# An edge-gated graph layer on one Trainium2 core: aggregation in quarter-width column tiles of TensorE instead of half-width ones

## The chip, the cores and the metric

The kernel runs on one core of a Trainium2 chip. The time is device time of one launch, in microseconds, as the median of the runs; the profile is one execution of the same program recorded by the hardware profiler. Engines are named as in the profile: PE is TensorE's matmul, PEld its weight load, DVE is VectorE, ACT is ScalarE, POOL is GpSimd, SP is SyncE.

## The reference: what is computed

The inputs are `x` (16 batches, 1024 nodes, 256 features) and one sparse matrix `adj` (1024 x 1024, the same for all batches, 9,052 entries that are not zero, 8.8 for a target on average, 19 at most). `adj` stands for both matrices of the layer. Cut to what matters:

```python
pre_u = jnp.einsum('bud,dk->buk', h_t, W1[:d])
pre_v = jnp.einsum('bvd,dk->bvk', h_t, W1[d:])
hidden = jax.nn.relu(pre_u[:, :, None, :] + pre_v[:, None, :, :] + b1)
S = jax.nn.sigmoid(jnp.einsum('buvk,ko->buvo', hidden, W2)[..., 0] + b2[0])
a_t = jnp.einsum('buv,bud->bvd', S * A_a, h_t)
m_t = jnp.einsum('uv,bud->bvd', A_m, h_t) * h_t
z_t = beta1 * h_t + beta2 * (a_t @ Wa + ba) + beta3 * (m_t @ Wm + bm)
```

Only the entries (edges) of `adj` that are not zero count. For each edge from a source u to a target v and each batch there is one gate S; each target sums its sources' rows twice, with weight `adj` (for m) and with weight S times `adj` (for a).

## The kernel before

**Tiling.** The 16 batches go in 4 groups of 4 (`GB`). A block `k` is one group with one tile of 128 targets, so there are 32 blocks. A block has two windows of 64 targets (`W`), and the edges of a window lie in 5 edge tiles (`TW`) of 128 slots each. One pass of the main loop, a step `n`, is one edge tile of one block: 10 steps a block, 320 in all, 64 windows.

**Which edge goes where.** `lists(vt)` sorts each target's edges into the slots. The 64 targets of a window are two halves of 32 (`V`): the lower half fills the slots from the start, the upper half from the end, so the lower half's edges lie in tiles 0, 1, 2 and the upper half's in tiles 2, 3, 4 (`HALVES`). A target's first slot comes from prefix sums that PE makes of the counts (L235 with the fixed matrix `ahead`, L236 with `below`), then from a few DVE operations on one column (L239 to L248). For each edge, `onehot` says which of the half's 32 targets it belongs to (L295).

**A step.** POOL gathers one row of 8 KB an edge from a table in HBM (`fetch`, L480: the rows hold, for 4 batches, the product with W1 and the plain features), into one of 5 buffers `fetched`. PE spreads the targets' product to the edges (`expand`, L494, into `pc`, two buffers). DVE adds the two (`gate`, L510), then does relu, times W2 and the sum for each of 4 batches (L514). ACT makes the weights: `left_adj` (L503) writes one-hot times `adj` for 4 batches, and after the sigmoid (L517) four instructions write the same times the gate (L520). Then `aggregate` (L531) multiplies: the stationary operand is 128 edges x 64 columns (32 targets with weight `adj`, 32 with weight S times `adj`), the moving one is 128 edges x 256 features, one matmul for each batch and each half that the tile has edges of. Two batches share a bank of `acc` side by side: a matmul of 64 columns takes one half of PE's columns, so batches 0 and 1 write partitions 0 to 63 and batches 2 and 3 write partitions 64 to 127; a window has 6 pairs of tile and half, 24 matmuls. These are float32 matmuls, and the trace shows each as two records; L494, in the type fp32r, is shown as one.

**Behind a half.** After tile 2 the lower half is done, after tile 4 the upper one: ACT copies `acc` out (`half_end`, L540), PE turns it over (`turn_over`, L550), ACT copies that to `LT` (L552), DVE multiplies by the targets' own features (`times_h`, L561). `block_end` (L578, L582) multiplies by the two weight matrices and adds. In each block `halves` (L347 with `w_v`, L381, L382, L390, L393) prepares the next block's targets, and in some steps `rows` (L347 with `w_u`, L363) prepares a tile of the table.

**The order of work.** It is written out by hand (`manual_schedule`), and each engine runs its instructions in that order. On PE a step `n` is: `aggregate(n-1)`, then what else the step has (turning over, `block_end`, `halves`, `rows`), then `expand(n+2)`. On DVE it is `gate(n)` and what was put off to it. On POOL, `fetch(n+4)` stands behind `aggregate(n-1)`, whose buffer it takes. On ACT: the copy out of `acc`, the sigmoid, L520 four times, `left_adj(n+1)`.

**Start and end.** The first 95.6 us sort the first edges and fill the first tables. The last window is finished in pieces (`tail`, L606 to L620): for 32 targets at a time it multiplies four batches side by side, in matmuls whose stationary operand is 128 x 32 (the forms `128*32` of L613).

Of the kernel before, what the change touches and what calls it, by code (L numbers as in the profile page):

```python
# [13 lines left out]
P = 128  # L14
# [3 lines left out]
def kernel(  # L18
# [40 lines left out]

    nc = tc.nc  # L60
# [11 lines left out]
    V = 32  # L72
    HALVES = [[0], [0], [0, 1], [1], [1]]
    OFF = [0, V, 2 * V, 4 * V, 5 * V, 6 * V]
    RC = 5 + S
    BIG = float(N * N)
    assert D == 256 and DC == 2 and NW == 2 and S % 8 == 0
# [49 lines left out]

    inw = fixed([P, 1], "inw")
    nc.vector.scalar_tensor_tensor(inw, late, -float(W), row, ALU.mult, ALU.add)
    upper = fixed([P, 1], "upper")  # L130
    nc.vector.tensor_scalar(upper, inw, float(V), None, ALU.is_ge)
    lower = fixed([P, 1], "lower")
    nc.vector.tensor_scalar(lower, inw, float(V), None, ALU.is_lt)
    MID = TW // 2
    until = fixed([P, 1], "until")
    nc.vector.tensor_scalar(until, upper, float((TW - 1 - MID) * P), float((MID + 1) * P), ALU.mult, ALU.add)
    since = fixed([P, 1], "since")
    nc.vector.tensor_scalar(since, upper, float(MID * P), None, ALU.mult)
    base = fixed([P, 1], "base")
    nc.vector.tensor_scalar(base, upper, float(E), None, ALU.mult)  # L140
# [3 lines left out]
    ahead = fixed([P, P], "ahead")  # L144
    below = fixed([P, P], "below")
    hv = fixed([P, 2 * NW, 1], "hv")
    for q in range(2 * NW):
        nc.vector.tensor_tensor(hv[:, q, :], late if q // 2 else soon, upper if q % 2 else lower, ALU.mult)
    nc.vector.memset(below, 0.0)
    for q in range(2 * NW):  # L150
        c = slice(q * V, (q + 1) * V)
        nc.vector.tensor_scalar(ahead[:, c], upto[:, c], row, hv[:, q, :], ALU.is_le if q % 2 else ALU.is_gt, ALU.mult)
        if q % 2:
            nc.vector.tensor_scalar(ahead[:, c], ahead[:, c], -1.0, None, ALU.mult)
            nc.vector.tensor_copy(below[:, c], hv[:, q - 1, :].to_broadcast([P, V]))
# [8 lines left out]
    place = fixed([P, 2, V], "place")  # L164
    nc.vector.tensor_copy(place.rearrange("p k v -> p (k v)"), upto[:, :W])
# [20 lines left out]
    onehot = const.tile([P, NT * NW, OFF[TW]], mybir.dt.bfloat16, name="onehot")  # L186
# [25 lines left out]
    def lists(vt):  # L212
# [22 lines left out]
        nc.tensor.matmul(pw[:, 0:1], ahead, R[:, 0:1], start=True, stop=True)  # L235
        nc.tensor.matmul(pw[:, 1:2], below, R[:, 0:1], start=True, stop=True)  # L236
        yield
        first = R[:, 1:2]
        nc.vector.tensor_tensor(first, pw[:, 0:1], base, ALU.add)  # L239
        from_ = wk.tile([P, 1], FP, name="from", bufs=4)  # L240
        nc.vector.tensor_tensor(from_, pw[:, 1:2], since, ALU.max)
# [51 lines left out]
        for q in range(2):  # L293
            j = slice(q * MID, q * MID + MID + 1)
            nc.vector.tensor_tensor(  # L295
                onehot[:, sl, q * 3 * V:(q + 1) * 3 * V].rearrange("p w (j v) -> p w j v", j=3),
                place[:, q, :].unsqueeze(1).unsqueeze(1).to_broadcast([P, NW, 3, V]),
                col[:, :, j, 4:5].to_broadcast([P, NW, 3, V]), ALU.is_equal)
# [199 lines left out]
    def left_adj(n):  # L498
        k, g, vt, w, j = where(n)
        i = vt * NW + w  # L500
        m = len(HALVES[j])
        lefts[n] = wk.tile([P, m, GB, 2, V], FP, name=f"left{m}", bufs=3 if m == 1 else 1)
        nc.scalar.activation(lefts[n][:, :m, :, 0, :],  # L503
                             onehot[:, i, OFF[j]:OFF[j + 1]].rearrange("p (q v) -> p q v", q=m).unsqueeze(2)
                             .to_broadcast([P, m, GB, V]), AF.Copy, scale=val[:, i, j:j + 1])
# [336 lines left out]
```

## Time and profile before

| what | value |
|---|---|
| median of 3 runs | 1288.98 us (1284.83 to 1293.57) |
| the profiled execution's own time | 1292.69 us |
| its span, from the first to the last instruction | 1290.8 us |
| mean granted TensorE clock over the span | 0.971 |
| first and last `gate` addition on DVE (L510) | 95.6 us, 1268.9 us |
| L514 on DVE, 1280 times | 471.0 us, 423 ns each |
| L510 on DVE, 320 times | 389.2 us, 1216 ns each |
| L494 on PE, 640 times | 247.5 us, 468 ns each |
| L578 on PE, 992 records | 260.9 us, 392 and 379 ns each |

A record of a PE matmul covers its passage through the array, so records overlap: what one costs in a row of them is read from the distance between starts, not from its length. A clock of 1.00 in a row means that TensorE was granted its full clock there. In a list of waits, the columns are the microseconds in total, how often, and the longest. In a table by windows, the number behind an engine's busy time counts its instructions.

### The profile page before, as it was taken

How to read it: one execution, taken by the hardware profiler on the slowest of the kernel's cores; microseconds unless marked ns; L12 is line 12 of the kernel's file. 1: busy time of each engine (PE TensorE's matmuls, PEld its weight loads, DVE VectorE, ACT ScalarE, POOL GpSimd, SP SyncE). 2: the span in 40 equal slices, each digit the busy share in tenths (PEclk: the TensorE clock that was granted, in tenths of full speed). 3: DMA queues.
4: the chain of work that ended last, by engine and by line, in shares of the span. 5: the costliest groups of instructions: out<-in, count | busy, mean ns of one | idle time of the engine just before them, and what ended most of it. 6: DMA issues, size and time to landing. Idle time of an engine off the chain costs nothing. (4 is left out here: it accounts for less than half of the span.)

```text
span 1290.8 us, 21720 instructions
## 1 busy us (share of the span) xinstructions
PE 1193.6 (92%) x6641; PEld 795.9 (62%) x6641; DVE 1089.6 (84%) x3421; ACT 880.4 (68%) x2567; POOL 413.3 (32%) x412
## 2 busy tenths in 40 slices
PE   3838999998979989999999999999999999999996
PEld 3625666665646656666666666666666666666654
DVE  7539878899899888888888898888778999899994
ACT  2426676676757667777777777777677777777773
POOL 0045642352624415222222232222222333233330
PEclk9868999999989989999999999999999999999999
DMA  9469998897898979999998899999998989898892
GB/s 301 154 187 339 313 344 286 279 337 245 280 317 302 341 270 304 332 341 341 335 326 321 323 331 322 318 321 381 345 317 301 338 311 315 297 322 315 318 324 98
DMA packets 151967, 393.37 MB, mean 305 GB/s; under 512 B 16816, under 2 KB 110512, under 8 KB 115632
## 3 DMA queue, kind: packets, MB, share of 16 engines
q0 software_dynamic: 49504, 299.85, 64.7%
q1 hardware_dynamic: 81552, 72.89, 17.5%
q10 hardware_dynamic: 20784, 19.14, 4.8%
q8 instruction: 55, 0.90, 0.3%
q14 instruction: 72, 0.59, 0.1%
HBM read 395.88 MB, written 50.33 MB: 346 GB/s over the span
## 5 line engine op out<-in xcount | busy, mean ns | idle before, releaser
L480 POOL DMA_INDIRECT fetched<-table,uidx x320 | 325.6, 1018 | 747.6 <-PE acc L531 444.5
L514 DVE SCALAR_TENSOR_TENSOR t<-t,w_b 128x256 f32<-128x256 f32 x1280 | 471.0, 423 | 19.4 <-DVE t L510 0.5
L510 DVE TENSOR_TENSOR t<-fetched,pc 128x1024 f32<-128x1024 f32 x320 | 389.2, 1216 | 108.1 <-PE pc L494 69.4
L531 PE MATMUL acc<-fetched,left 128*64 128x256 f32 x3072 | 420.1, 394 | 11.8 <-ACT left L520 11.7
L531 PEld LDWEIGHTS acc<-fetched,left 128*64 128x64 f32 x3072 | 201.7, 138 | 203.2 <-issue 52.1
L520 ACT ACTIVATE left<-left,gt 128x32 f32<-128x32 f32 (+1 forms) x1280 | 313.5, 315 | 10.7
L494 PE MATMUL pc<-X,mark 128*128 128x512 f32 x640 | 247.5, 468 | 19.5 <-DVE t L510 16.5
L517 ACT ACTIVATE gt<-sc,b_b 128x4 f32<-128x4 f32 x320 | 95.2, 297 | 137.2 <-DVE t L514 135.4
L347 PE MATMUL misc<-w_u,hT 128*128 128x256 f32 x512 | 129.3, 401 | 22.6 <-DMA hT<-in_xT_dram 11.7
L494 PEld LDWEIGHTS pc<-X,mark 128*128 128x128 f32 x640 | 118.6, 193 | 40.4 <-DVE t L510 21.0
L503 ACT ACTIVATE left<-onehot,val 128x128 f32<-128x128 bf16 (+1 forms) x320 | 130.3, 407 | 7.8 <-DMA val<-in_adjT_dram,vidx 7.8
L578 PE MATMUL misc<-w_m,LT 128*128 128x256 f32 x496 | 133.6, 392 | 0.0
L540 ACT COPY ev<-acc 128x512 f32<-128x512 f32 x128 | 75.0, 586 | 79.2 <-PE acc L531 79.1
L578 PE MATMUL misc<-w_a,LT 128*128 128x256 f32 x496 | 127.3, 379 | 0.0
L347 PEld LDWEIGHTS misc<-w_u,hT 128*128 128x128 f32 x512 | 97.9, 199 | 43.7 <-issue 11.7
L347 PE MATMUL misc<-w_v,hT 128*128 128x256 f32 x512 | 124.1, 386 | 0.0
L578 PEld LDWEIGHTS misc<-w_m,LT 128*128 128x128 f32 x496 | 88.8, 189 | 33.1 <-issue 23.8
L347 PEld LDWEIGHTS misc<-w_v,hT 128*128 128x128 f32 x512 | 99.8, 195 | 13.8
L305 POOL DMA_INDIRECT val<-in_adjT_dram,vidx x80 | 83.3, 1042 | 76.3 <-DVE eq L280 51.7
L514 DVE DVE_READ_ACCUMULATOR t<-t,w_b 128x1 f32 x1280 | 103.8, 81 | 0.0
L393 ACT CAST X<-misc 64x512 fp32r<-64x512 f32 x128 | 74.4, 581 | 42.7 <-PE misc L390 38.5
L578 PEld LDWEIGHTS misc<-w_a,LT 128*128 128x128 f32 x496 | 94.2, 190 | 12.8
(127 smaller groups left out, 843.0 us busy)
## 6 DMA issues: line engine op xcount, KB each, us to landing
hT<-in_xT_dram SPq DMA_DIRECT2D x40, 512.0 KB, 10.4
table<-in_x_dram ACTq DMA_DIRECT2D x32, 512.0 KB, 8.8
table<-tab SPq DMA_DIRECT2D x32, 512.0 KB, 5.2
h_blk<-in_x_dram SPq DMA_DIRECT2D x31, 512.0 KB, 12.5
out_dram<-h_blk SPq DMA_DIRECT2D x31, 512.0 KB, 5.7
fetched<-table,uidx POOLq DMA_INDIRECT x320, 7.6
key<-in_adjT_dram POOLq DMA_DIRECT2D x6, 512.0 KB, 8.7
whose<-few ACTq DMA_DIRECT2D x32, 40.0 KB, 4.5
```

Of the source, the lines that this page charges most:

```text
L305: nc.gpsimd.indirect_dma_start(out=val[:, i, j:j + 1], out_offset=None, in_=adj_flat, in_offset=bass.IndirectOffsetOnAxis(ap=vidx[:, i, j: ...
L347: nc.tensor.matmul(p[:, bb * D:(bb + 1) * D], hT[:, 2 * h + bb, i, :], wt[:, i, :], start=(i == 0 and not begun), stop=(i == DC - 1), skip ...
L480: nc.gpsimd.indirect_dma_start(out=fetched[n % NF], out_offset=None, in_=table[g], in_offset=bass.IndirectOffsetOnAxis(ap=uidx[:, vt * NW ...
L494: nc.tensor.matmul(pcs[n][:, c], marks[n // TW][:, j * P:(j + 1) * P], cuts[k][:, w, c], start=True, stop=True)
L503: nc.scalar.activation(lefts[n][:, :m, :, 0, :], onehot[:, i, OFF[j]:OFF[j + 1]].rearrange("p (q v) -> p q v", q=m).unsqueeze(2) .to_broad ...
L510: nc.vector.tensor_tensor(t, fetched[n % NF][:, :GD].rearrange("p (b d) -> p b d", b=GB), pcs.pop(n).rearrange("p (b d) -> p b d", b=GB), ...
L514: nc.vector.scalar_tensor_tensor(t[:, b, :], t[:, b, :], 0.0, w2_b, ALU.max, ALU.mult, accum_out=sc[:, b:b + 1])
L517: nc.scalar.activation(gt, sc, AF.Sigmoid, bias=b2_b)
L520: nc.scalar.activation(lefts[n][:, :m, b, 1, :], lefts[n][:, :m, b, 0, :], AF.Copy, scale=gt[:, b:b + 1])
L531: nc.tensor.matmul(accs[q][half * 2 * V:(half + 1) * 2 * V, pair, :], left[:, i, b].rearrange("p k v -> p (k v)"), f[:, GD + b * D:GD + (b ...
L540: nc.scalar.copy(evs[q], accs.pop(q))
L578: nc.tensor.matmul(pz[:, bb * D:(bb + 1) * D], LTs[k][:, bb, c, h, i, :], wt[:, c, :], start=False, stop=(i == 1 and c == DC - 1), skip_gr ...
```

## The change

The half of 32 targets is replaced by a quarter of 16 (`V` is now 16, `Q` is 4, and `U` is the 32 of before). A matmul of `aggregate` has 32 stationary columns (16 targets with each of the two weights), takes a quarter of PE's columns, and the four batches write the four quarters of the partitions of one bank. Quarter q may have edges in tiles q and q+1 (`QUARTERS`), so a window has 8 pairs of tile and quarter, 32 matmuls. Two quarters share a bank (`h, r = divmod(q, 2)`): quarter 0 and 1 the first 256 and the last 256 columns of `acc0`. All else on the path is laid out anew for this: `onehot` has 8 x 16 columns a window and not 6 x 32, `left` is one kind of tile with three buffers (before: three of one size and one of the other), `LT` has another order of its dimensions, and the sorting in `lists` has four prefix sums and not two, with two more DVE operations on one column. On this input every edge still finds a slot in its quarter's tiles, and the rows gathered are as many as before: 9,052 for each group of batches.

```diff
-    V = 32
-    HALVES = [[0], [0], [0, 1], [1], [1]]
+    U = W // 2
+    Q = 4
+    V = W // Q
+    QUARTERS = [[0], [0, 1], [1, 2], [2, 3], [3]]
...
-        nc.tensor.matmul(pw[:, 0:1], ahead, R[:, 0:1], start=True, stop=True)
-        nc.tensor.matmul(pw[:, 1:2], below, R[:, 0:1], start=True, stop=True)
+        for i in range(4):
+            nc.tensor.matmul(pw[:, i:i + 1], sums[:, i].rearrange("p w q v -> p (w q v)"), R[:, 0:1],
+                             start=True, stop=True)
         yield
         first = R[:, 1:2]
-        nc.vector.tensor_tensor(first, pw[:, 0:1], base, ALU.add)
         from_ = wk.tile([P, 1], FP, name="from", bufs=4)
-        nc.vector.tensor_tensor(from_, pw[:, 1:2], since, ALU.max)
+        nc.vector.tensor_scalar(from_, pw[:, 1:2], base, low_, ALU.add, ALU.max)
+        nc.vector.scalar_tensor_tensor(first, from_, high_, pw[:, 0:1], ALU.min, ALU.add)
+        nc.vector.tensor_scalar(from_, pw[:, 2:3], second_, since, ALU.add, ALU.max)
+        nc.vector.tensor_tensor(from_, pw[:, 3:4], from_, ALU.max)
...
-        for q in range(2):
-            j = slice(q * MID, q * MID + MID + 1)
+        for i in range(2):
             nc.vector.tensor_tensor(
...
-        m = len(HALVES[j])
-        lefts[n] = wk.tile([P, m, GB, 2, V], FP, name=f"left{m}", bufs=3 if m == 1 else 1)
+        m = len(QUARTERS[j])
+        o = max(2 * j - 1, 0)
+        lefts[n] = wk.tile([P, 2, GB, 2, V], FP, name="left")
...
-        for i, q in enumerate(HALVES[j]):
-            first = j == (MID if q else 0)
+        for i, q in enumerate(QUARTERS[j]):
+            h, r = divmod(q, 2)
+            first = j == h * MID and r == 0
             if first:
-                accs[q] = psa.tile([P, 2, D], FP, name=f"acc{q}")
-            for b in (0, 2, 1, 3):
-                half, pair = divmod(b, 2)
-                nc.tensor.matmul(accs[q][half * 2 * V:(half + 1) * 2 * V, pair, :],
+                accs[h] = psa.tile([P, 2, D], FP, name=f"acc{h}")
+            for b in range(GB):
+                nc.tensor.matmul(accs[h][b * 2 * V:(b + 1) * 2 * V, r, :],
                                  left[:, i, b].rearrange("p k v -> p (k v)"), f[:, GD + b * D:GD + (b + 1) * D],
-                                 start=(first and pair == 0), stop=(j == (TW - 1 if q else MID)),
-                                 skip_group_check=True)
+                                 start=first, stop=(j == q + 1), skip_group_check=True)
...
-        nc.scalar.copy(LT.rearrange("p a c b k v -> p (a c b k) v")[:, :, v], pt.rearrange("p (i v) -> p i v", v=V))
+        v = slice(w * W + q * U, w * W + (q + 1) * U)
+        r = (w * W + q * U) // V
+        nc.scalar.copy(LT.rearrange("p c b k (r v) -> p r (c b k) v", v=V)[:, r:r + 2],
+                       pt.rearrange("p (r i v) -> p r i v", r=2, v=V))
```

On PE, in a block of the later part of the program, tiles 0 to 2 of a window stand like this before (a name like acc or fetched is a buffer, the size is the output's):

```order
L531 MATMUL acc_6940<-fetched_173,left_6891 64x256 x4
L578 MATMUL misc<-w_m,LT 128x256 x2
L578 MATMUL misc<-w_a,LT 128x256 x2
L494 MATMUL pc<-X,mark 128x512 x2
L531 MATMUL acc_6940<-fetched_174,left_6928 64x256 x4
L550 MATMUL misc<-ident,ev_6843 128x128 x4
L550 MATMUL misc<-ident,ev_6913 128x128 x4
L390 MATMUL misc<-low,swap 128x512
L494 MATMUL pc<-X,mark 128x512 x2
L531 MATMUL acc_6940<-fetched_175,left_6961 64x256 x4
L531 MATMUL acc_7019<-fetched_175,left_6961 64x256 x4
L494 MATMUL pc<-X,mark 128x512 x2
```

and in the changed kernel, where L531 has become L554, L578 L602, L550 L572, L494 L517 and L390 L413:

```order
L554 MATMUL acc_7223<-fetched_176,left 32x256 x4
L602 MATMUL misc<-w_m,LT 128x256 x2
L602 MATMUL misc<-w_a,LT 128x256 x2
L517 MATMUL pc<-X,mark 128x512 x2
L554 MATMUL acc_7223<-fetched_177,left 32x256 x8
L572 MATMUL misc<-ident,ev_7122 128x128 x4
L572 MATMUL misc<-ident,ev_7196 128x128 x4
L413 MATMUL misc<-low,swap 128x512
L517 MATMUL pc<-X,mark 128x512 x2
L554 MATMUL acc_7223<-fetched_178,left 32x256 x4
L554 MATMUL acc_7306<-fetched_178,left 32x256 x4
L517 MATMUL pc<-X,mark 128x512 x2
```

Nothing changes its place; tile 1 (and tile 3, not shown) has eight matmuls where it had four, tiles 0, 2 and 4 have as many as before, and all are 32 columns wide.

On ACT, tiles 0 to 2 of a window before (ev is the copy of acc, L520 the four gated weights of a tile, L503 the one-hot weights of the next tile):

```order
L520 ACTIVATE left_5414<-left_5414,gt 128x32 x4
L503 ACTIVATE left_5451<-onehot,val 128x4x32
L517 ACTIVATE gt<-sc,b_b 128x4
L520 ACTIVATE left_5451<-left_5451,gt 128x32 x4
L503 ACTIVATE left_5484<-onehot,val 128x8x32
L487 CAST mark<-whose 128x640
L517 ACTIVATE gt<-sc,b_b 128x4
L520 ACTIVATE left_5484<-left_5484,gt 128x2x32 x4
L503 ACTIVATE left_5515<-onehot,val 128x4x32
```

and in the changed kernel (L520 has become L543, L503 L527, L517 L540, L487 L510):

```order
L543 ACTIVATE left<-left,gt 128x16 x4
L527 ACTIVATE left<-onehot,val 128x8x16
L540 ACTIVATE gt<-sc,b_b 128x4
L543 ACTIVATE left<-left,gt 128x2x16 x4
L527 ACTIVATE left<-onehot,val 128x8x16
L510 CAST mark<-whose 128x640
L540 ACTIVATE gt<-sc,b_b 128x4
L543 ACTIVATE left<-left,gt 128x2x16 x4
L527 ACTIVATE left<-onehot,val 128x8x16
```

The instructions are as many and stand in the same order; three tiles of five now write 32 columns with each gate, where four wrote 32 and one wrote 64, and two write 16.

More of the change, by code (lines that the diff above doesn't have):

```diff
@@ L145 @@
[L145 to L155, printed above, removed]
+    low_ = fixed([P, 1], "low_")
@@ new lines @@
+    nc.vector.tensor_scalar(low_, mine[:, 1:2], float(P), None, ALU.mult)
+    second_ = fixed([P, 1], "second_")
+    nc.vector.tensor_scalar(second_, mine[:, 2:3], float(P), None, ALU.mult)
+    high_ = fixed([P, 1], "high_")
+    nc.vector.tensor_scalar(high_, second_, -1.0, float(E), ALU.mult, ALU.add)
+    sums = fixed([P, 4, NW, Q, V], "sums")
+    ahead = sums[:, 0].rearrange("p w q v -> p (w q) v")
+    same = hv.rearrange("p w q one -> p (w q) one").to_broadcast([P, NW * Q, V])
+    nc.vector.memset(sums[:, 1:], 0.0)
```

68 lines of the change are left out of this document (39 added, 29 removed).

## The prediction

> **What bounds the kernel now.** I read the page first, for who is busy:
>
> ```profile
> PE 1193.6 (92%) x6641; PEld 795.9 (62%) x6641; DVE 1089.6 (84%) x3421; ACT 880.4 (68%) x2567; POOL 413.3 (32%) x412
> DMA  9469998897898979999998899999998989898892
> GB/s 301 154 187 339 313 344 286 279 337 245 280 317 302 341 270 304 332 341 341 335 326 321 323 331 322 318 321 381 345 317 301 338 311 315 297 322 315 318 324 98
> HBM read 395.88 MB, written 50.33 MB: 346 GB/s over the span
> ```
>
> PE is the busiest, but DVE and the 16 DMA engines are close behind. An average over stages decides nothing, so next comes the table by windows, cut at the first addition of `gate` (95.6), the start of block 10 (507.3, from where no edges are sorted), the end of block 30 (1240.6), and once more inside the long stretch:
>
> ```profile
> core 0: us, PE busy (x) PEld busy (x) DVE busy (x) ACT busy (x) POOL busy (x), PEclk, DMA share, GB/s
> 0.00:95.60 95.60, 49.44 (x193) 40.30 (x193) 50.35 (x139) 32.67 (x44) 16.48 (x22) 0.83 0.69 211
> 95.60:507.30 411.70, 378.33 (x2041) 249.49 (x2043) 368.24 (x1164) 273.99 (x802) 174.72 (x170) 0.96 0.88 307
> 507.30:1240.60 733.30, 726.95 (x4130) 482.81 (x4130) 639.25 (x2020) 550.23 (x1646) 214.84 (x215) 1.00 0.92 324
> 1240.60:1290.80 50.20, 38.88 (x282) 23.30 (x279) 31.76 (x99) 23.51 (x77) 7.25 (x7) 0.94 0.54 182
> ...
> 507.30:865.60 358.30, 355.40 (x2019) 237.03 (x2019) 308.79 (x973) 266.72 (x795) 104.69 (x106) 1.00 0.92 325
> 865.60:1010.10 144.50, 143.54 (x808) 97.42 (x810) 118.67 (x376) 105.43 (x312) 39.14 (x39) 1.00 0.95 335
> 1010.10:1240.60 230.50, 228.01 (x1307) 148.35 (x1303) 211.79 (x673) 178.09 (x540) 71.00 (x71) 1.00 0.89 316
> ```
>
> From 507.3 to 1240.6 PE is busy 726.95 of 733.3 us at full clock: PE sets the pace there, for 57% of the span. Behind it stand DMA (0.92) and DVE (639.25, 87%). From 95.6 to 507.3 nobody is full: PE 92%, DVE 89%, DMA 0.88. Third, the waits, DVE's from 507.3 to 1240.6, then PE's there, then DVE's from 95.6 to 507.3:
>
> ```profile
> DVE t L510 <- PE pc L494: 50.6, 56, 2.6
> DVE low L382 <- ACT X L381: 13.6, 14, 1.0
> DVE t L510 <- DMA fetched<-table,uidx: 8.7, 12, 1.2
> ...
> PE misc L390 <- ACT LT L552: 5.0, 21, 0.2
> PE acc L531 <- ACT left L520: 1.3, 2, 0.8
> ...
> DVE t L510 <- DMA fetched<-table,uidx: 24.0, 6, 16.7
> DVE t L510 <- PE pc L494: 18.2, 18, 2.0
> ```
>
> In the long stretch DVE waits 50.6 us for PE, and PE waits 6.3 us for ACT. That is the picture of a PE that others follow.
>
> [...]
>
> **The aggregation on PE.** [...] Timeline of PE, a tile with one half, the middle tile with two, and the tail, where 32-column matmuls already run four abreast:
>
> ```profile
> 600.13 1.08 PE L531 MATMUL acc<-fetched,left 128*64 128x256 f32 x8
> 601.14 0.50 PE L351 MATMUL misc<-bias_p,unit 128*128 128x512 f32 x1
> ...
> 592.00 1.95 PE L531 MATMUL acc<-fetched,left 128*64 128x256 f32 x16
> 593.88 0.50 PE L351 MATMUL misc<-bias_p,unit 128*128 128x512 f32 x1
> ...
> 1277.61 1.07 PE L613 MATMUL misc<-w_m,LT 128*32 128x256 f32 x16
> 1278.50 1.05 PE L613 MATMUL misc<-w_a,LT 128*32 128x256 f32 x16
> 1279.47 0.38 PE L606 MATMUL misc<-bias_p,unit 128*128 128x256 f32 x1
> ```
>
> Eight records take 1.01 us, sixteen 1.88 us. They run two abreast (64 columns each), so eight more records are four more rounds, and a round is (1.88 - 1.01) / 4 = 0.217 us. In the tail 32 records take 1279.47 - 1277.61 = 1.86 us: as long as eight rounds, so there are four abreast. At that price a tile with one quarter (8 records, two rounds) takes 1.86 - 6 x 0.217 = 0.56 us and a tile with two quarters (16 records, four rounds) 1.86 - 4 x 0.217 = 0.99 us. A window took 4 x 1.01 + 1.88 = 5.92 us and will take 2 x 0.56 + 3 x 0.99 = 4.09 us: 1.83 us less. The saving sits in tiles 0, 2 and 4; tiles 1 and 3 cost what they did. There are 64 windows (L487, once a window, has 64 instructions):
>
> ```profile
> L487 ACT CAST mark<-whose 128x640 fp32r<-128x640 uint8 x64 | 45.4, 709 | 0.0
> L510 DVE TENSOR_TENSOR t<-fetched,pc 128x1024 f32<-128x1024 f32 x320 | 389.2, 1216 | 108.1 <-PE pc L494 69.4 <-DMA fetched<-table,uidx 32.7 <-PE misc L390 1.3
> L480 POOL DMA_INDIRECT fetched<-table,uidx x320 | 325.6, 1018 | 747.6 <-PE acc L531 444.5 <-DVE t L510 216.7 <-DVE t L514 37.7
> ```
>
> So 117 us of PE work go. The unknown is whether four streams that read four different rows of features run abreast as in the tail, where four matmuls read one weight. Bounds: two abreast as in L531 today (8 x 4 rounds a window and not 24, so 8 x 0.217 = 1.74 us more), and four as in L613. I take four: L531's two streams already read different features at the full pace of 0.217.
>
> **What of it reaches the end.** A stretch cannot get shorter than what its other engines need.
>
> From 507.3 on there are 42 windows, 77 us of PE work. In 507.3 to 865.6 DMA is busy 0.92 of 358.3: at a share of 1.00 it needs 330 us, a ceiling of 28.7 us on the gain (PE's: 20 windows, 37). In 865.6 to 1010.1 it is 0.95, a ceiling of 7.2 us. In 1010.1 to 1240.6 DVE is the nearest: 211.79 us busy, and up to 11 us that it loses between its own instructions and to ACT (of the whole stretch's 94 idle us, 51 were PE's and 9 the gather's; the other 34, over 733 us, are 11 in 230), of which the wait for ACT will shrink with PE's. So it needs 219 to 223 us, a ceiling of 8 to 12; I take 12. Sum of the ceilings: 48. None is reached exactly, because fetches have only five buffers and a transfer that comes late is not made up: DVE waits for the gather now already, at times,
>
> ```profile
> 1079.02 1.22 DVE L510 TENSOR_TENSOR t<-fetched,pc 128x1024 f32<-128x1024 f32 x1 [0.81 <-DMA fetched<-table,uidx]
> fetched<-table,uidx POOLq DMA_INDIRECT x320, 7.6
> ```
>
> and a gather takes 7.6 us from issue to landing, more than two steps of 3.5. I take 40 of the 48. What is late next: DVE's additions, behind the gather, and no longer behind `pc`.
>
> From 95.6 to 507.3 there are 20 windows, 37 us of PE work, but DVE waits for PE's `pc` only 18.2 us there; that is the ceiling, and the gather's 24.0 stay. I take 12. The sorting's cost comes off it: two more DVE operations for each of 8 tiles of targets,
>
> ```profile
> L239 DVE TENSOR_TENSOR R<-misc,base 128x1 f32<-128x1 f32 x6 | 0.9, 151 | 0.2 <-PE misc L236 0.2
> L235 PE MATMUL misc<-R,ahead 128*128 128x1 f32 x12 | 2.7, 298 | 0.3 <-DVE R L239 0.3
> L520 ACT ACTIVATE left<-left,gt 128x32 f32<-128x32 f32 x1024 | 245.3, 310 | 8.5
> L520 ACT ACTIVATE left<-left,gt 128x64 f32<-128x64 f32 x256 | 68.2, 337 | 2.1
> L503 ACT ACTIVATE left<-onehot,val 128x128 f32<-128x128 bf16 x256 | 98.8, 386 | 7.8 <-DMA val<-in_adjT_dram,vidx 7.8
> L503 ACT ACTIVATE left<-onehot,val 128x256 f32<-128x256 bf16 x64 | 31.6, 493 | 0.0
> ```
>
> 8 x 2 x 0.15 = 2.4 us, of which 2 of 8 tiles lie in the prologue; and four prefix matmuls for two, 2 x 2 more records of at most 0.3 us for each tile, in all 8 x 4 x 0.3 = 9.6 us of PE if nothing overlapped. Six tiles of them (7 us) fall in this stretch, where PE has just been freed of 37 us; two fall in the prologue (2.4 us at most). I take 2 us here and 1 us in the prologue, with the constants made there; the ends are 0 and 12 together.
>
> From 1240.6 there are two windows, 3.7 us of PE work, and the last tile's matmuls are on the path to the end: 2 us.
>
> Edits that I cost at nothing. ACT gets lighter: the gated weights fall from 4 x 4 x 310 + 4 x 337 ns a window to at most 20 x 310, the one-hot ones from 4 x 386 + 493 to at most 5 x 386 ns, together 0.2 us or more; ACT is at 75% in the long stretch, so this is hidden, and it covers the copies into `LT`, which move 512 elements in 16-element pieces where they had 32; were each a half slower, 128 x 0.3 = 38 us would go on ACT, still under PE's time. `left`, now with three buffers for all tiles, is free again after one step. POOL's and SP's queues keep their order and bytes, so each fetch is only issued earlier, behind an earlier `aggregate`.
>
> Sum: 40 + 12 - 2 - 1 + 2 = 51 us. Against the profiled execution's 1292.7 this gives 1241.7 us. That execution lies 0.3% above the median of the runs, 1289.0; a new median is by the same measure **1238 us**.
>
> **Rivals.** *A, the transfers hold.* If the DMA engines do not go over the share of 0.95 that they held from 865.6 to 1010.1, 358.3 us at 0.92 become 347 (11 gained), the next stretch gains nothing, the third its 12, the first perhaps 5: 28 us, so 1261. For it: gathers that DVE waits for, 346 GB/s of HBM over the span. Against it: one slice of 32 us moved 381 GB/s, above all three stretches' 316 to 335. [...]
>
> *B, slower: the quarters do not run abreast.* If four different moving operands share the array's inputs so that only two run at once, a window costs 1.74 us more; over 42 windows where PE is the bound that is 73 us, and some 35 in the first stretch: 1395 us. It decides at 64 / 24 = 2.67 abreast, where 64 records of a window take the 24 rounds of today. Against it: the tail's 1.86 us for 32 records.
>
> *C, no change.* PE is only followed closely, and DVE or the gather's round trip (five buffers) sets the pace, so the freed time turns into waits: 1289. Against it: the 50.6 us for which DVE waits for PE.
>
> *D, all of PE's part comes out.* DMA takes the higher load without delay and the long stretch loses 64 us (77 less 13 for DVE's own), the first 18, the end 3, less 3: 82 us, 1207.
>
> **Chances and range.** My forecast 0.58, A 0.22, D 0.10, C 0.05, B 0.05. The range from 1212 to 1264 takes in the forecast and A and leaves out B, C and most of D. A measurement of this kernel can tell about 1% (13 us) from no change. Faster by more: the forecast, D and nearly all of A, 0.88; within 1%: C and the rest of A, 0.07; slower: 0.05.
>
> **What would show it.** In the changed kernel's timeline a run of 8 records of the aggregation should reach the next line in 0.56 us and one of 16 in 0.99 us; 1.0 and 1.9 mean B. The PE share from 507 on should fall from 99% to about 94%, DVE's rise to 92%, DMA's to 0.97. DVE's wait for `pc` should shrink from 50.6 us to under 20, that for the gather grow from 8.7. If the gather's wait takes over and DMA stays at 0.92, the round trip and not the rate is the limit. The forecast is wrong if the prologue, before the first addition on DVE, ends more than 2 us later than 95.6.

## The result, and the profile after

| | median | lowest to highest | runs |
|---|---|---|---|
| before | 1291.28 us | 1284.83 to 1293.84 | 4 |
| changed kernel | 1237.93 us | 1232.65 to 1250.19 | 4 |

The ratio is 0.9608, with a 95% interval of 0.9522 to 0.9693: 53 us less in the medians. A second set on another chip (six runs of the changed kernel, eleven of the one before; the experiment `e5_again` below) gave 0.9602 (0.9572 to 0.9631). The run that was profiled took 1250.19 us, span 1248.4 us, and is the slowest of its four; where it differs from the others is shown below, and so the span of `e5_again`, 1237.6 us, stands beside it.

The page of the changed kernel, its lines as in the page of before:

```profile
PE 1118.9 (90%) x7697; PEld 729.6 (58%) x7697; DVE 1089.3 (87%) x3438; ACT 851.2 (68%) x2567; POOL 415.4 (33%) x412
...
HBM read 395.88 MB, written 50.33 MB: 357 GB/s over the span
```

PE lost 75 us of busy time and DVE none: now they are three points apart. The bytes are the same. The table by windows, cut at the first addition of `gate`, the start of block 10 and the end of block 30, and the long stretch in three, at the starts of blocks 20 and 24 (columns as before: us, PE, PEld, DVE, ACT, POOL busy, clock, DMA share, GB/s):

```profile
0.00:95.50 95.50, 53.27 (x205) 43.53 (x205) 51.49 (x145) 32.71 (x44) 16.66 (x22) 0.80 0.70 212
95.50:499.50 404.00, 361.58 (x2385) 234.83 (x2387) 370.81 (x1176) 265.38 (x803) 174.80 (x170) 0.93 0.89 312
499.50:1199.40 699.90, 668.33 (x4803) 430.59 (x4796) 635.31 (x2019) 530.51 (x1645) 216.59 (x215) 0.99 0.94 340
1199.40:1248.40 49.00, 35.70 (x312) 20.63 (x311) 31.65 (x99) 22.57 (x77) 7.39 (x7) 0.94 0.55 189
499.50:839.10 339.60, 321.59 (x2305) 208.82 (x2301) 302.93 (x963) 254.03 (x787) 105.64 (x105) 0.98 0.93 341
839.10:977.00 137.90, 135.40 (x977) 89.50 (x970) 121.54 (x384) 104.55 (x320) 39.83 (x40) 1.00 0.98 360
977.00:1199.40 222.40, 211.34 (x1527) 132.27 (x1528) 210.84 (x672) 171.94 (x540) 71.12 (x70) 1.00 0.91 326
```

Against before, the four stretches are 0.1, 7.7, 33.4 and 1.2 us shorter: 42.4 us of span. Inside the long stretch the prediction cut the kernel before at 865.6, 4.8 us and more than a step behind the start of block 20; its first two parts cut at the same place of the program as here are:

```profile
507.30:860.80 353.50, 350.60 (x1990) 233.86 (x1992) 305.02 (x963) 263.98 (x787) 103.70 (x105) 1.00 0.92 327
860.80:1010.10 149.30, 148.34 (x838) 100.60 (x840) 122.44 (x385) 108.17 (x321) 40.13 (x40) 1.00 0.93 330
```

The last 222.40 us of the long stretch of the changed kernel have DVE busy for 210.84, as many us as before: there DVE has come level with PE (211.34). In the first part of it (339.60) PE is still the busiest, but no longer without gaps. The same stretch in `e5_again`:

```profile
498.40:1188.70 690.30, 664.23 (x4803) 429.14 (x4795) 635.28 (x2019) 530.20 (x1645) 216.71 (x215) 1.00 0.95 345
```

Here it is 43.0 us shorter than before's 733.3, and the sum over all four stretches is 1290.8 - 1237.6 = 53.2 us, the 53 of the medians.

The aggregation on the timeline of PE, changed kernel (start, us, line; what a run costs is the distance from its start to the next line's start, as in the numbers for before):

```profile
565.28 1.07 PE L554 MATMUL acc<-fetched,left 128*32 128x256 f32 x16
566.28 0.66 PE L572 MATMUL misc<-ident,ev 128*128 128x128 f32 x4
...
569.06 0.64 PE L554 MATMUL acc<-fetched,left 128*32 128x256 f32 x8
569.63 0.50 PE L374 MATMUL misc<-b_p,unit 128*128 128x512 f32 x1
...
577.49 1.07 PE L554 MATMUL acc<-fetched,left 128*32 128x256 f32 x16
578.49 0.51 PE L374 MATMUL misc<-bias_p,unit 128*128 128x512 f32 x1
```

Eight records take 0.57 us, sixteen 1.00 us: two rounds and four rounds at 0.217 us. In the run of sixteen at 565.28 four records start within the first 0.04 us, and no fifth within 0.20 us: four streams with four different rows of features run abreast.

The waits of DVE in the changed kernel's long stretch (us in total, times, longest):

```profile
DVE t L533 <- PE pc L517: 25.2, 21, 7.0
DVE t L533 <- DMA fetched<-table,uidx: 13.3, 17, 2.0
```

The wait for `pc` is half of before's 50.6, the wait for the gather is up from 8.7. One of these waits took 7.0 us; in `e5_again` none takes over 2.1. The timeline of PE there:

```profile
799.65 3.75 PE L370 MATMUL misc<-w_u,hT 128*128 128x256 f32 x8 [5.33 <-DMA hT<-in_xT_dram]
802.84 1.41 PE L517 MATMUL pc<-X,mark 128*128 128x512 f32 x2
804.18 1.54 PE L554 MATMUL acc<-fetched,left 128*32 128x256 f32 x16
805.65 0.55 PE L572 MATMUL misc<-ident,ev 128*128 128x128 f32 x3
```

A load of `hT`, the features that `rows` needs for the table, came late and held PE for 5.33 us; behind it the sixteen records take 805.65 - 804.18 = 1.47 us instead of 1.00. The granted clock, the number before the last two, was 0.56 there:

```profile
799.60:806.00 6.40, 6.35 (x29) 4.14 (x30) 1.68 (x4) 1.92 (x7) 0.00 (x0) 0.56 0.06 22
```

In `e5_again` PE waits for `hT` once in the long stretch, 1.4 us. This explains part of the 10.8 us between the two spans.

### The profile page after: what moved, and what is told of

It reads as the page before. It is cut to its first block, busy times and chain, and to the rows that moved or that the text cites. A ratio compares the mean times of both kernels' runs of the same rounds, so it can differ in the third digit from the quotient of the medians.

```text
span 1248.4 us, 23873 instructions
## 1 busy us (share of the span) xinstructions
PE 1118.9 (90%) x7697; PEld 729.6 (58%) x7697; DVE 1089.3 (87%) x3438; ACT 851.2 (68%) x2567; POOL 415.4 (33%) x412
## 5 line engine op out<-in xcount | busy, mean ns | idle before, releaser
L503 POOL DMA_INDIRECT fetched<-table,uidx x320 | 327.2, 1023 | 703.0 <-PE acc L554 500.8
L537 DVE SCALAR_TENSOR_TENSOR t<-t,w_b 128x256 f32<-128x256 f32 x1280 | 469.7, 422 | 19.8 <-DVE t L533 0.5
L554 PE MATMUL acc<-fetched,left 128*32 128x256 f32 x4096 | 324.0, 397 | 25.5 <-ACT left L543 25.3
L543 ACT ACTIVATE left<-left,gt 128x32 f32<-128x32 f32 (+1 forms) x1280 | 299.4, 304 | 10.4
L517 PE MATMUL pc<-X,mark 128*128 128x512 f32 x640 | 249.3, 471 | 19.5 <-DVE t L533 16.5
L554 PEld LDWEIGHTS acc<-fetched,left 128*32 128x32 f32 x4096 | 120.9, 110 | 191.9 <-issue 69.2
L540 ACT ACTIVATE gt<-sc,b_b 128x4 f32<-128x4 f32 x320 | 95.4, 298 | 197.1 <-DVE t L537 195.4
L370 PE MATMUL misc<-w_u,hT 128*128 128x256 f32 x512 | 132.2, 408 | 28.2 <-DMA hT<-in_xT_dram 16.9
L517 PEld LDWEIGHTS pc<-X,mark 128*128 128x128 f32 x640 | 119.5, 195 | 41.4 <-DVE t L533 18.3
L602 PE MATMUL misc<-w_m,LT 128*128 128x256 f32 x496 | 134.6, 394 | 0.0
L370 PEld LDWEIGHTS misc<-w_u,hT 128*128 128x128 f32 x512 | 100.3, 204 | 50.5 <-issue 18.5
L602 PE MATMUL misc<-w_a,LT 128*128 128x256 f32 x496 | 128.2, 381 | 0.0
L370 PE MATMUL misc<-w_v,hT 128*128 128x256 f32 x512 | 125.4, 389 | 0.0
L527 ACT ACTIVATE left<-onehot,val 128x128 f32<-128x128 bf16 (+1 forms) x320 | 116.6, 364 | 8.5 <-DMA val<-in_adjT_dram,vidx 8.5
L602 PEld LDWEIGHTS misc<-w_m,LT 128*128 128x128 f32 x496 | 89.5, 190 | 35.3 <-issue 25.9
L370 PEld LDWEIGHTS misc<-w_v,hT 128*128 128x128 f32 x512 | 100.6, 196 | 14.0
L537 DVE DVE_READ_ACCUMULATOR t<-t,w_b 128x1 f32 x1280 | 103.9, 81 | 0.0
L602 PEld LDWEIGHTS misc<-w_a,LT 128*128 128x128 f32 x496 | 94.8, 191 | 13.1
L562 ACT COPY ev<-acc 128x512 f32<-128x512 f32 x128 | 74.9, 585 | 30.1 <-PE acc L554 30.1
L572 PE MATMUL misc<-ident,ev 128*128 128x128 f32 x512 | 81.4, 290 | 11.6 <-DVE h_blk L606 10.8
## 6 DMA issues: line engine op xcount, KB each, us to landing
table<-in_x_dram ACTq DMA_DIRECT2D x32, 512.0 KB, 10.7
```

Of the source, the lines that this page charges most:

```text
L370: nc.tensor.matmul(p[:, bb * D:(bb + 1) * D], hT[:, 2 * h + bb, i, :], wt[:, i, :], start=(i == 0 and not begun), stop=(i == DC - 1), skip ...
L503: nc.gpsimd.indirect_dma_start(out=fetched[n % NF], out_offset=None, in_=table[g], in_offset=bass.IndirectOffsetOnAxis(ap=uidx[:, vt * NW ...
L517: nc.tensor.matmul(pcs[n][:, c], marks[n // TW][:, j * P:(j + 1) * P], cuts[k][:, w, c], start=True, stop=True)
L527: nc.scalar.activation(lefts[n][:, :m, :, 0, :], onehot[:, i, o:o + m, :].unsqueeze(2).to_broadcast([P, m, GB, V]), AF.Copy, scale=val[:, ...
L537: nc.vector.scalar_tensor_tensor(t[:, b, :], t[:, b, :], 0.0, w2_b, ALU.max, ALU.mult, accum_out=sc[:, b:b + 1])
L540: nc.scalar.activation(gt, sc, AF.Sigmoid, bias=b2_b)
```

## The experiments

Kernels that are compared by a ratio ran on the same chip as the runs of before beside them. Times are medians, and a single run is called so. The first theory was: PE's saving is real, and what is lost of it goes to the gather's round trip with five buffers and to DVE. The rivals: the rate of the transfers; the order in which PE takes its matmuls; late loads of `hT`.

**Do four streams need neighbours of different columns in the order of the matmuls?** In tiles 1, 2 and 3, which have two quarters, the loops over quarter and batch change places, so that each batch's two matmuls, which go to the same quarter of the columns, stand next to each other.

```diff
         for i, q in enumerate(QUARTERS[j]):
...
-            for b in range(GB):
+            if j == q // 2 * MID and q % 2 == 0:
+                accs[q // 2] = psa.tile([P, 2, D], FP, name=f"acc{q // 2}")
+        for b in range(GB):
+            for i, q in enumerate(QUARTERS[j]):
```

> The changed kernel with one thing undone: in a tile with two quarters the 8 matmuls are issued batch by batch (both quarters of a batch, which use the same quarter of PE's columns, one behind the other) instead of quarter by quarter. Theory: the saving comes from neighbours in the queue that lie in different columns; a run of 16 records then takes about ten rounds of 0.217 us and 0.14 us, 2.3 us, where it took 0.99, and with 3 such tiles in 64 windows the time goes to 1400 us or more. Rival: PE sorts the matmuls by column itself, or narrower columns alone make them cheap; then 0.99 us and 1238 us as before.

A single run took 1241.16 us, with before at 1290.05. Its timeline of PE:

```profile
573.51 1.09 PE L555 MATMUL acc<-fetched,left 128*32 128x256 f32 x16
574.53 0.50 PE L374 MATMUL misc<-b_p,unit 128*128 128x512 f32 x1
```

Sixteen records still take 1.02 us, against 1.00. The theory behind the experiment fell: the saving is there in this order too, where neighbours share their columns.

**Is it being abreast that pays, or being narrow?** All four batches of a pair of tile and quarter go to the same quarter of the columns, with as many records of the same shape; two pairs of one tile go to two quarters. The sums are then not the layer's.

```diff
-                nc.tensor.matmul(accs[h][b * 2 * V:(b + 1) * 2 * V, r, :],
+                c = 2 * r + j - q
+                nc.tensor.matmul(accs[h][c * 2 * V:(c + 1) * 2 * V, b % 2, :],
...
-                                 start=first, stop=(j == q + 1), skip_group_check=True)
+                                 start=(b == 0), stop=(b == GB - 1), skip_group_check=True)
```

> The changed kernel, but the four batches of a tile and quarter go to the same quarter of PE's columns (another quarter for each tile), two into each half of the bank; as many matmuls, as narrow, with the same operands, but their sums are not the layer's. The batch-by-batch run showed that the order in the queue does not matter, so what is left of the theory is: four different column quarters run at once, and a narrow matmul alone is no cheaper. Then 8 records take eight rounds, 0.14 + 8 x 0.217 = 1.87 us where 0.56, and 16 records (two columns) the same 1.88 where 0.99; a window costs 9.4 us and not 4.1, and with 64 windows on PE the time is near 1540 us. Rival: the cost goes with the columns loaded, and 32 columns take half of 64; then 0.56 and 0.99 stay, 1238 us.

A single run took 1617.42 us, where about 1540 was expected, on a chip where before takes 1309.3. Its timeline of PE:

```profile
704.83 1.91 PE L555 MATMUL acc<-fetched,left 128*32 128x256 f32 x8
706.68 1.13 PE L603 MATMUL misc<-w_m,LT 128*128 128x256 f32 x4
...
709.06 2.81 PE L555 MATMUL acc<-fetched,left 128*32 128x256 f32 x16
711.80 0.87 PE L573 MATMUL misc<-ident,ev 128*128 128x128 f32 x6
```

Eight records in one quarter of the columns take 1.85 us where they take 0.57 abreast. With the 0.14 us by which a run of eight went beyond its four rounds before (1.01 - 4 x 0.217), a round costs (1.85 - 0.14) / 8 = 0.214 us, as much as the 0.217 of a round of two records of 64 columns before: here a matmul of 32 columns was no cheaper than one of 64, and all of the gain is in being abreast. Sixteen records in two quarters took 2.74 us, where 1.88 was expected; the starts of such a run stand at the end.

**Is the gather late, in the changed kernel and before?** Half of the sources are left out of each gather, so it lands sooner (5.8 us after issue, in `e5_again` 7.8) and moves half the bytes; the instructions stay.

```diff
-            bounds_check=N - 1, oob_is_err=False)
+            bounds_check=N // 2 - 1, oob_is_err=False)
```

> The changed kernel, but the gather skips the sources from 512 on, so half of its rows are not fetched (their old contents are used) and its traffic of 300 MB is halved. Theory: transfers only add waits behind PE and DVE, which hold most of the time: 15 to 30 us less than 1238, about 1215. Rival A (the transfers hold): 45 us less or more, under 1193.

> The kernel before with the same half gather. Theory: PE sets the pace from 507 us on, so only the gather's waits before that come out: 10 to 25 us less than 1290, about 1273, and less than the changed kernel gains by the same edit. Rival A: the gain is as large as or larger than that of the changed kernel.

The changed kernel takes 1219.92 us (1218.06 to 1220.2), ratio 0.9446 (0.9406 to 0.9486); before, with the same edit, 1280.36 us, ratio 0.9927 (0.9905 to 0.995). So the gather costs the changed kernel some 20 us against `e1_serial` and `e5_again`, and the kernel before 10. Of these, 11.4 us lie in the long stretch of the changed kernel (690.3 to 678.9) and 3.9 in that of before (733.3 to 729.4). It does not tell the rate from the round trip, since both are relieved.

**Is DVE late?** L537 (relu, times W2, sum) works on half of the features, in the changed kernel and in the one before.

```diff
-            nc.vector.scalar_tensor_tensor(t[:, b, :], t[:, b, :], 0.0, w2_b,
+            nc.vector.scalar_tensor_tensor(t[:, b, :D // 2], t[:, b, :D // 2], 0.0, w2_b[:, :D // 2],
```

> The changed kernel, but relu and sum for the gate (four instructions a step) cover half of the features, which takes some 0.13 us off each of 1280 instructions, 170 us of DVE. Theory: DVE is what holds from 977 us on and much of 95 to 500 us, so the first loses 10 to 16 us (to PE's 30 us a block) and the second 15 to 30: about 1200. Rival (PE or the transfers hold everywhere, DVE nowhere): less than 10 us.

> The kernel before with relu and sum over half of the features. Theory: from 507 us on PE held it, so the lighter DVE gives nothing there, and 10 to 20 us before: about 1275, a smaller gain than the 28 us of the changed kernel. Rival: DVE held the kernel before too; then 25 us or more come off.

The changed kernel takes 1211.29 us, ratio 0.9383 (0.9344 to 0.9423), some 29 us less than `e1_serial` and `e5_again`; about 1200 was expected. Against `e5_again` the stretch ahead of block 10 is 24.2 us shorter (405.1 to 380.9), but the long one only 1.7 (690.3 to 688.6). Its part from block 24 on loses 5.3 us (221.9 to 216.6), not the 10 to 16 expected, and blocks 20 to 23 take 9.2 us more (137.9 to 147.1). In the long stretch DVE waits for the gather far longer than the 8.7 us of `e5_again`, and in blocks 20 to 23 PE waits for a late load of `hT`:

```profile
DVE t L533 <- DMA fetched<-table,uidx: 39.1, 36, 2.9
...
PE misc L370 <- DMA hT<-in_xT_dram: 8.3, 1, 8.3
```

Before takes 1275.32 us, ratio 0.9884 (0.9865 to 0.9902), 15 us less, and its long stretch shows where these 15 us are not:

```profile
493.90:1222.90 729.00, 723.81 (x4123) 481.25 (x4124) 533.08 (x2019) 548.42 (x1644) 214.05 (x215) 1.00 0.93 326
```

With 106 us less of DVE work the stretch went from 733.3 to 729.0 us, and its first block, block 10, starts 507.3 - 493.9 = 13.4 us sooner instead. Before the change DVE did not set the pace of the long stretch; it did hold what lies ahead of it.

**The rate, or the round trip?** A sixth buffer leaves every byte where it is and gives a gather more time to land. Its room comes from what the change freed and from three trims.

```diff
-    NF = 5
+    NF = 6
...
-        lefts[n] = wk.tile([P, 2, GB, 2, V], FP, name="left")
+        lefts[n] = wk.tile([P, 2, GB, 2, V], FP, name="left", bufs=2)
...
-        s_of = wk.tile([P, M], FP, name="s_of", bufs=2)
+        s_of = wk.tile([P, M], FP, name="s_of", bufs=1)
...
-        k_of = wk.tile([P, M], FP, name="k_of", bufs=2)
+        k_of = wk.tile([P, M], FP, name="k_of", bufs=1)
```

> The changed kernel as it is, as the measure for the two beside it: 1232 to 1250 us, 0.96 of the kernel before.

> The changed kernel with six gather buffers instead of five (room is made by two buffers for the weights' tile instead of three and one instead of two for two small columns of the sorting). Theory: the round trip of a gather (7 to 9 us with 5 buffers and 3.2 us a step) is what makes DVE wait behind it, 13 us from 500 us on and some 8 us before: 8 to 15 us less than the changed kernel. Rival (rate): the DMA engines are full there, a sixth buffer only makes the queue longer: within 4 us of it, or a little slower.

The changed kernel as it is takes 1240.58 us (1234.38 to 1244.3), with six buffers 1223.08 us (1217.86 to 1226.52), ratio 0.9468 (0.9441 to 0.9495): 17.5 us less, a little more than the 8 to 15 expected, with intervals that do not meet. No work is left out, and it is faster than both kernels. DVE's waits over the whole span, with five buffers:

```profile
DVE t L533 <- DMA fetched<-table,uidx: 34.9, 23, 17.2
```

and with six:

```profile
DVE t L533 <- DMA fetched<-table,uidx: 17.0, 2, 16.8
```

What is left with six is the first gather of all. Its table by windows, the three parts of the long stretch and the whole of it:

```profile
495.60:818.20 322.60, 316.79 (x2308) 206.60 (x2304) 302.22 (x963) 254.22 (x787) 105.51 (x105) 1.00 0.98 358
818.20:955.50 137.30, 135.40 (x977) 89.70 (x970) 121.53 (x384) 104.42 (x320) 39.95 (x40) 1.00 1.00 364
955.50:1173.20 217.70, 211.43 (x1527) 132.48 (x1526) 210.83 (x672) 171.83 (x540) 70.99 (x70) 1.00 0.93 334
495.60:1173.20 677.60, 663.61 (x4803) 428.77 (x4795) 634.58 (x2019) 530.48 (x1645) 216.44 (x215) 1.00 0.97 351
```

The first part took 353.5 us before and takes 322.6 now, 30.9 of PE's 37 us; the second took 149.3 and takes 137.3, 12.0 of PE's 15. The first part's bytes move at 358 GB/s where they moved at 327, with a DMA share of 0.98. A sixth buffer, with all of the bytes, takes 12.7 us off the long stretch, and half of the bytes with five buffers took 11.4: the rate was no limit; the time to land, with five buffers, was.

The other way round, one buffer less, in the changed kernel and before (`NF = 4`), on the chip where before takes 1309.3 us:

> The changed kernel with four gather buffers instead of five. Theory: the round trip (gate 2.6, weights 1.4, aggregation 0.6 to 1.0, issue 1.0, landing 7 to 8 us: 13 us) over four steps is 3.3 us a step, more than the 3.25 and 3.11 that PE and DVE need, so all blocks from 500 us on get longer by 1 to 4 us and the time is 1265 to 1300 us, with DVE waiting for the gather in most steps. Rival (rate): within 8 us of 1240.

> The kernel before with four gather buffers. Theory: its steps of 3.58 us hide the round trip of 13 us over four steps (3.3), but not where steps are 3.3 already and where transfers crowd; it loses less than the changed kernel does, 10 to 35 us on 1290. Rival (rate): no change. If it loses as much as the changed kernel, the round trip held the kernel before already.

The changed kernel takes 1343.74 us, ratio 1.0238 (1.0184 to 1.0293); before 1383.47 us, ratio 1.0544 (1.0474 to 1.0613). DVE's wait for the gather, in the changed kernel and in before:

```profile
DVE t L533 <- DMA fetched<-table,uidx: 125.7, 76, 17.1
...
DVE t L510 <- DMA fetched<-table,uidx: 154.4, 99, 17.0
```

Both lost far more than I expected of them. With four buffers the round trip sets the pace of both kernels, and the change then gains 3%. Before lost 5.4%, nearly as much as the changed kernel; by the sign set for this run, the round trip would have held it with five buffers already. `e3_half_gather_before` does not bear that out: relieved of half its bytes, the long stretch of before lost 3.9 us. So the run shows that four buffers are too few for both, and not what held before with five. Before with six buffers was not run, so it is not shown how much of the 17.5 us a sixth buffer would have given without the change. In shares of before, the changed kernel stands at 1.0238, 0.9602 and 0.9468 with four, five and six buffers (the first on another chip than the other two): the steps are 6.4% and 1.3%.

**Are late loads of `hT` a part of it?** One more buffer for them, and twelve of the loads issued four or five steps earlier.

```diff
-    hts = main.enter_context(tc.tile_pool(name="hts", bufs=NT + 2))
+    hts = main.enter_context(tc.tile_pool(name="hts", bufs=NT + 3))
...
-    loads.update(zip((74, 80, 86, 90, 113, 123, 133, 143), ((2, vt) for vt in range(NT))))
+    loads.update(zip((74, 80, 86, 90, 108, 118, 128, 138), ((2, vt) for vt in range(NT))))
...
-    loads.update(zip((173, 183, 193, 203, 206, 209, 214, 223), ((3, vt) for vt in range(NT))))
+    loads.update(zip((168, 178, 188, 198, 202, 205, 209, 218), ((3, vt) for vt in range(NT))))
```

> The changed kernel with the loads of hT for the second half of the batches put 4 or 5 steps earlier in SP's queue (one more buffer for hT). Theory: with PE faster these loads come too late at times (one wait of 5.3 us on PE, with a drop of the clock behind it, in the profiled execution), so the wait on PE for hT goes and the time is 3 to 8 us less than the changed kernel, and scatters less. Rival: it was one bad moment; within 2 us, or slower since the loads now meet other transfers.

1235.49 us (1231.73 to 1237.89), ratio 0.957 (0.9546 to 0.9594). That is 5 us under `e5_again`, but the two intervals overlap: inconclusive. In its profiled run PE never waits for `hT` in the long stretch; that of `e5_again` lost only 1.4 us to it, so this wait alone is not the 5 us. The 8.3 us of `e4_light_dve` show that such a load comes late in other runs too. That late loads cost the profiled run time is seen in its timeline; what they cost the median is not settled.

**Do the gather and DVE together account for the loss?** Six buffers and the light DVE at once.

> The changed kernel with six gather buffers and with relu and sum over half of the features, so that neither the gather's round trip nor DVE holds. Theory: what is left is PE, with its whole saving out where it was the bound: 32.1 us a block where it has table rows to make and 30.1 us in blocks 24 to 30, 20 us less than with six buffers alone from 95 to 500 us: about 1192 us. If something else holds (the rate of the transfers, ACT), the blocks stay at 32.5 and 31.1 and the time over 1212.

1183.98 us (1181.59 to 1185.18), ratio 0.9172 (0.9152 to 0.9191): 107 us less than before, 91 us less than `e12_light_dve_before` on the same chip. Its long stretch:

```profile
470.30:1137.30 667.00, 654.03 (x4799) 422.62 (x4798) 531.32 (x2020) 533.19 (x1645) 213.04 (x216) 1.00 0.98 357
```

and the waits of DVE there:

```profile
DVE t L533 <- PE pc L517: 71.9, 67, 3.3
DVE low L405 <- ACT X L404: 24.6, 23, 1.5
```

PE is busy 654.03 of 667.0 us, DVE waits for it again, and there is no wait for the gather. A block takes 32.2 us in blocks 10 to 19, 33.9 in 20 to 23 and 29.9 from 24 on, where 32.1 and 30.1 were expected. The stretch is 62 us shorter than the one of `e12_light_dve_before`, which has the same light DVE.

## Why the prediction was right, and which step was not

**The aggregation on PE: right.** Predicted 0.56 and 0.99 us for runs of 8 and 16 records, measured 0.57 and 1.00. The tail's 32-column matmuls were the right row to price it by, though there the four share one weight.

**The total: right, 51 us predicted, 53 measured.** By parts, with the profiled run and then `e5_again`: the long stretch gained 33.4 and 43.0 us (predicted 40), the one ahead of it 7.7 and 6.6 (predicted 12 less 2), the start 0.1 and 2.3 (predicted a loss of 1), the end 1.2 and 1.3 (predicted 2). That 51 and 53 lie so close is luck: the profiled run alone gained 42.4, and the runs of the changed kernel spread over 17.5 us.

**The ceiling from the transfers: wrong.** This is the step that failed: "at a share of 1.00 it needs 330 us, a ceiling of 28.7 us on the gain", and 7.2 us for the next part by the same rule, 35.9 together. The two parts took 502.8 us before. With six buffers they take 322.6 + 137.3 = 459.9 us, 42.9 less: 7 us more than the two ceilings allow, at shares of 0.98 and 1.00. (The sum of both is compared since the cut between them lay 4.8 us late.) Here the share of busy DMA time was not a measure of the work that has to be done: for the same bytes the first part, up to block 20, was busy for 0.92 x 353.5 = 325 us before, for 0.93 x 339.6 = 316 us in the changed kernel, and for 0.98 x 322.6 = 316 us with six buffers. So the busy time fell with the change itself, and not with the sixth buffer; why it fell is open. The error did not show in the total, because the sentence behind it ("fetches have only five buffers and a transfer that comes late is not made up") took 8 us off a ceiling that was too low, where it should have taken about 13 off a higher one: from five to six buffers the long stretch goes from 690.3 to 677.6 us. So the number was right by luck here, with the weights of two causes mixed up.

**DVE at the end of the stretch: right in size, and reached only without the late gathers.** Predicted that DVE needs 219 to 223 us from block 24 on; the part took 222.4 in the profiled run and 217.7 with six buffers, 1.3 us under that bound, with DVE busy 210.83 of it, 97%. That DVE holds it there is shown by `e11_six_buffers_light_dve`: a lighter DVE took 677.6 - 667.0 = 10.6 us more off the long stretch, 8.2 of them from block 24 on (217.7 to 209.5), and PE again became the one that is waited for.

**Where the 77 us of PE work in the long stretch went**, then: 43.0 us come out with five buffers, 12.7 more with a sixth, 10.6 more with a lighter DVE. Of the 10.7 us left, 6.6 are idle time of PE, which grew from 6.4 to 13.0 us; the other 4 are not accounted for. A light DVE alone is worth 733.3 - 729.0 = 4.3 us there without the change, so that its 10.6 are not wholly a part of PE's 77.

**The stretch ahead of block 10: too much was taken.** The ceiling was DVE's wait for `pc`, 18.2 us, of which 12 were taken. The wait fell to 9.7 us and that for the gather stayed, at 25.0. Of the gather's 24.0 us before, 16.7 are the wait for the first gather of all, which ends with the first addition at 95.6 and so lies in the prologue; only 7.3 us of it stood in this stretch, and 7.9 in the changed kernel (25.0 less 17.1). `e12_light_dve_before` shows why little of PE's 37 us comes out here: a lighter DVE brings block 10 forward by 13.4 us even in the kernel before, and `e4_light_dve` makes this stretch 24.2 us shorter in the changed one. To this stretch the change adds DVE work, and that term was mis-sized. The list of lines of the changed kernel, DVE, the four operations of the sorting that replace two (mean ns behind the busy time):

```profile
L264 DVE TENSOR_SCALAR from<-misc,second__112,since 128x1 f32<-128x1 f32 x6 | 1.7, 277 | 0.2
L262 DVE TENSOR_SCALAR from<-misc,base,low__110 128x1 f32<-128x1 f32 x6 | 1.6, 272 | 0.0
L263 DVE SCALAR_TENSOR_TENSOR R<-from,high__114,misc 128x1 f32<-128x1 f32 x6 | 1.3, 216 | 0.2
L265 DVE TENSOR_TENSOR from<-misc,from 128x1 f32<-128x1 f32 x6 | 0.9, 158 | 0.2
```

Together they take 0.92 us for a tile of targets, where two operations of 0.15 stood: 8 x 0.62 = 5 us, not 2.4. Six of the eight tiles lie in this stretch: 3.7 us where 2 were taken, and DVE's busy time there rose by 2.6 us (368.24 to 370.81). That is about half of the 2 to 3 us that are missing against the forecast of 10. I had counted the operations that were added and not that three of the four are of a longer kind.

**The edits at nothing: right.** The copies into `LT`, feared because they move 16 elements at a time, take 578 ns where they took 580, and ACT's busy time fell by 29 us.

**The signs to look for.** From block 10 on, PE is at 668.33 / 699.9 = 95% (predicted 94), DVE at 91% (92), DMA at 0.94 (0.97); in `e5_again` at 96%, 92% and 0.95. The wait for `pc` is 25.2 us in the profiled run and 17.4 in `e5_again` (predicted under 20), that for the gather 13.3 and 8.7. So it grew in one run and not in the other, and the sign that should have told the round trip from the rate ("If the gather's wait takes over and DMA stays at 0.92") told neither. The prologue ended at 95.5 us, so the sign that would have said the forecast is wrong did not come. Here late gathers cost more than DVE's own waits show: 8.7 us of waits in the long stretch of `e5_again` against the 12.7 us that a sixth buffer takes off it.

**The rivals.** A, the transfers hold at 0.95: refuted by the shares of 0.98 and 1.00 of `e6_six_buffers`, whose page says

```profile
HBM read 395.88 MB, written 50.33 MB: 365 GB/s over the span
```

where the page of before has 346, and by `e11_six_buffers_light_dve` with 377 GB/s. B, two abreast: refuted by 0.57 and 1.00 us, and `e8_one_column` shows how slow it is without being abreast. C, DVE or the round trip sets the pace already: refuted by `e12_light_dve_before`, whose long stretch shrank by 4.3 us when DVE lost 106 us of work, and by `e3_half_gather_before`, where it shrank by 3.9. D, all of PE's part: not with five buffers; six came nearer, at 1223.

## What to carry to other kernels

When the bounding engine gets lighter, ask of each follower by itself whether its rate or its delay will hold: here a DMA share of 0.92 did not tell how much shorter a stretch could get (353.5 us became 322.6, at 0.98), and a trial with one buffer more told at once that the delay held (12.7 us). If a change frees memory, spend it on the wait that comes next: here the sixth buffer was worth another third of the gain. No run shows whether it would have fitted before. In these runs a matmul of 32 stationary columns cost as much as one of 64 (0.214 and 0.217 us a round) where no other ran beside it, so count rounds, not matmuls.

## What was not expected of the hardware

**Two orders of the same columns, two costs.** In `e1_serial` the records for the same quarter stand side by side in the program, four at a time, and all sixteen take 1.02 us, where about 2.3 was expected. In `e8_one_column` eight records for one quarter stand ahead of eight for another, and the sixteen take 2.74 us. With a round of 0.217 us and the 0.14 us beyond the rounds, that is (2.74 - 0.14) / 0.217 = 12 rounds, neither the 8 of two streams side by side from the start nor the 16 of one after the other. The trace counts the records that begin in the first 0.89 us of such a run, and in 0.01 us more (window, PE and PEld busy and counts, clock, DMA share, GB/s):

```profile
709.06:709.95 0.89, 0.89 (x4) 0.47 (x5) 1.00 0.78 138
709.06:709.96 0.90, 0.90 (x6) 0.47 (x7) 1.00 0.77 137
```

Four records start in 0.89 us, 0.22 us for each, the pace of one stream; the next 0.01 us has two starts, which is read as a second stream. Four rounds of one, four of both and four of the other would make the 12; this split is an estimate from the 2.74 us and these counts. What sets the moment at which the second stream starts is not shown.

**The time was steep in the number of gather buffers.** From five to four the changed kernel lost 6.4% of before's time, from five to six it gained 1.3%.

**The granted clock was low behind one wait.** In the profiled run PE had no work for 5.33 us before 799.65 us, and from 799.6 to 806.0 us the granted clock was 0.56, where it was 1.00 from 780 to 794: eight records of L370 took 3.19 us, where they take 1.55 earlier in the same trace, and sixteen of the aggregation 1.47 us instead of 1.00. This is one place in one run; what set the clock there is not shown.
